# A transformer block with two expert layers: shared expert's blocks overlapped, first weight loads on other queues, three gathered rows a tile, 16 columns of places

## Chip, cores and metric

The kernel runs on one core of a Trainium2 chip, in one launch. The metric is the device time in microseconds; several runs are taken and the median is compared. The profile shown is one further execution, recorded by the hardware profiler.

## The reference

Input x has 4 sequences of 1024 tokens with 256 features, in float32. Four residual layers follow one another; each first normalizes its input over the features.

```
x = x + attn_a(layernorm(x))   # 16 heads of 16; rotary; per-head layernorm; scores ** 4, causal
x = x + ffn(layernorm(x))      # 16 experts of width 176, top 6, plus a shared expert of width 352
x = x + attn_b(layernorm(x))   # a convolution along the first axis, taps from p, q, beta, gamma; silu
x = x + ffn(layernorm(x))      # the same weights again

def ffn(xf):
    shared_out = silu_and_mul(xf @ shared_w1.T) @ shared_w2.T
    probs = softmax(xf @ gate_w.T)
    weights, selected = top_k(probs, 6)          # not renormalized
    moe_out = sum over selected experts of weight * (silu_and_mul(xf @ w1[e].T) @ w2[e].T)
    return moe_out + shared_out
```

attn_b sees the sequences as its first axis, so its convolution is over the four sequences.

## The kernel before

X, the residual stream, stays in SBUF for the whole run, as eight token tiles of 128 positions by four sequences. The tokens are cut into two groups g of four token tiles each.

**Start.** Constants are made on POOL (L137 to L189). SP loads the first half of X in four transfers of 512 KB, one for each sequence (`load_x`, L153). ACT issues eight loads of `w_qkv` of 96 KB and the two tables of rotary angles (L487 to L494). SP then issues 32 tiny loads that replicate the scale and bias of the per-head norm (`lns`, `lnb`, L497 to L502), `w_out`, the second half of X and the gate's weights. The lines outside the hand-ordered part are put in order by a planner, and so they need not run in the order of the text: in the profile `w_out` and one load of X's second half stand before `lns`.

**Attention** (L892 to L938) is ordered by hand: generators ("bites") in lanes are stepped between score blocks. It ends with the routing plan of group 0 and the scatter of its rows into the queue `xq` by indirect DMAs on POOL.

**Expert part** (L941 on). The rows of a group, copied six times each and sorted by expert, fill 111 tiles of 128 rows. `stream` (L1044) walks four stages of 111 tiles: the first expert layer for groups 0 and 1, the second for groups 0 and 1. For each tile, TensorE runs gate and up (`pgu`, L1107), the transposes of the hidden rows (`pht`, L1121), those of a later tile's input (`pxt`, L1076) and the down product (`py`, L1130); ACT and DVE make the activation (`hbuf`, L1115 and L1116), ACT copies out (`hT`, `xgT`, `yo`), and SP loads three tiles (`xg`) and stores three (`yq`) at a time. In the last stage the results go to their places in `z` by an indirect DMA each (L1141), with the row numbers in a column of `zi`; ACT writes a column (L1091), and the eight columns are used in turn. `yo` has two buffers of three tiles.

Beside the tiles, three lanes are stepped: QUEUE holds the weighted sum of the stage before (`combine`) and then the scatter of the stage after (`fill`); SIDE holds convolution, norm, gate and plan; FILL holds the shared expert (`shared`). `combine(g, n, ready)` issues, in each bite, n indirect gathers on POOL into one of three `yg` buffers (L1252), and runs the sums (L1231, on DVE) of the bite two before. A stage's `each` gives QUEUE one bite a tile, so with n = 2 the 96 gathers of a middle stage take 48 tiles, and with SIDE through, the scatter follows with three rows a tile. FILL gets one TensorE bite in each fourth tile.

**Shared expert.** `shared(g, i)` (L985) handles one token tile ("block"): norm on DVE (`hxn`), eight transposes (`hpt`) and two copies on ACT (`hxT`), three times gate and up (`pg`, `pu`), silu on ACT and a product on DVE (`hs`), and the down product in two halves (`po`), each added into X by DVE. All its PSUM tiles rotate through two buffers. For the first stage the four blocks run one after the other ahead of the stream (L1341 and L1342), in the middle stages beside the tiles, and for the last stage in a loop at the end (L1356 to L1361), in which each turn gives one bite to `combine(1, 3, last, True)` and one to FILL. There the rows come from `z` by plain loads on SP (L1250), and `last` finishes a block's FILL bites and stores the block. `Bites.add` (L56) runs a generator up to its first yield at the moment when it is added.

Of the kernel before, what the change touches and what calls it, by code (L numbers as in the profile page):

```python
# [8 lines left out]
FP = mybir.dt.float32  # L9
I32 = mybir.dt.int32  # L10
U32 = mybir.dt.uint32
AF = mybir.ActivationFunctionType
# [13 lines left out]
P = 128  # L26
B, N, E = 4, 1024, 256
# [7 lines left out]
TG = NT // NG  # L35
TT = TG * B
NTILE = TT * TOPK + NEXP - 1
LB = 3
# [68 lines left out]
def block_kernel(  # L107
# [20 lines left out]
    nc = tc.nc  # L128
# [5 lines left out]
    dram = ctx.enter_context(tc.tile_pool(name="dram", bufs=1, space=bass.MemoryType.DRAM))  # L134


    ident = const.tile([P, P], FP, name="ident")  # L137
    make_identity(nc, ident)
    ones = const.tile([P, P], FP, name="ones")
    nc.gpsimd.memset(ones, 1.0)  # L140
    eps_t = const.tile([P, 1], FP, name="eps_t")
    nc.gpsimd.memset(eps_t, EPS)


    X = const.tile([P, NT, B, E], FP, name="X")

    def load_x(l, t):
        nc.sync.dma_start(
            out=X[:, t : t + 4, l, :],
            in_=x[l, t * P : (t + 4) * P, :].rearrange("(t p) e -> p t e", p=P),  # L150
        )

    for l in range(B):  # L153
        load_x(l, 0)


    xq = [dram.tile([NTILE * P, E], FP, name=f"xq{g}") for g in range(NG)]
# [33 lines left out]
    def transpose4(psum_tile, src, cols, rows=P):  # L191

        for i in range(4):
            nc.tensor.transpose(  # L194
                psum_tile[0:rows, i * P : (i + 1) * P], src[:, i, cols], ident
            )
# [12 lines left out]
    def ln_apply(xs, dst, mv, rstd, n=4):  # L209

        for i in range(n):
            nc.vector.tensor_scalar(
                dst[:, i, :],
                xs[:, i, :],
                mv[:, i, 0:1],
                rstd[:, i : i + 1],
                ALU.subtract,
                ALU.mult,
            )
# [255 lines left out]
    with ExitStack() as actx:  # L475
# [10 lines left out]
        wout_sb = ap1.tile([P, 2, E], FP, name="wout_sb")  # L486
        for k in range(2):  # L487
            for g in range(4):
                nc.scalar.dma_start(
                    out=wqkv_sb[:, k, g // 2, :, g % 2, :],  # L490
                    in_=w_qkv[k * P : (k + 1) * P, g, :].rearrange("p (x c) -> p x c", x=3),
                )
        nc.scalar.dma_start(out=cos_sb, in_=cos16.rearrange("(t p) d -> p t d", p=P))
        nc.scalar.dma_start(out=sin_sb, in_=sin16.rearrange("(t p) d -> p t d", p=P))  # L494
        nc.gpsimd.memset(lns, 0.0)
        nc.gpsimd.memset(lnb, 0.0)
        for r in range(G):  # L497
# [443 lines left out]
    with ExitStack() as fctx:  # L941
# [34 lines left out]
        wgu_f = [wgu[:, k].rearrange("p n f -> p (n f)") for k in range(2)]  # L976
        w2_f = [w.rearrange("p n e -> p (n e)") for w in (w2a, w2b)]

        zi = fw.tile([P, 8], I32, name="zi")

        hbuf = [fw.tile([P, 2 * P], FP, name=f"hbuf{i}") for i in range(4)]
        for hb in hbuf:
            nc.vector.memset(hb[:, FI:], 0.0)

        def shared(g, i):  # L985

            t = g * TG + i
            yield "el"
            xn = f1.tile([P, 4, E], FP, name="hxn")
            ln_apply(  # L990
                X[:, t, :, :],
                xn,
                mvs[g][:, 4 * i : 4 * i + 4, :],
                rstds[g][:, 4 * i : 4 * i + 4],
            )
            xT = f1.tile([P, 2, 512], FP, name="hxT")
            yield "pe"
            for k in range(2):
                pt = ps_s.tile([P, 512], FP, tag="s", name="hpt")
                transpose4(pt, xn, slice(k * P, (k + 1) * P))  # L1000
                nc.scalar.copy(xT[:, k, :], pt)
            hs = []
            for s, rows in enumerate(S_ROWS):
                yield "pe"
                pg = ps_s.tile([P, 512], FP, tag="s", name="pg")
                pu = ps_s.tile([P, 512], FP, tag="s", name="pu")
                for dst, gu in ((pg, 0), (pu, 1)):
                    c = gu * FS + s * P
                    for k in range(2):
                        nc.tensor.matmul(  # L1010
                            dst[0:rows, :],
                            lhsT=sh1[:, k, c : c + rows],
                            rhs=xT[:, k, :],
                            start=(k == 0),
                            stop=(k == 1),
                        )
                h = f1.tile([P, 512], FP, name=f"hs{s}")
                nc.scalar.activation(h[0:rows, :], pg[0:rows, :], AF.Silu)
                nc.vector.tensor_mul(h[0:rows, :], h[0:rows, :], pu[0:rows, :])
                hs.append(h)  # L1020
            for pr in range(2):
                yield "pe"
                po = ps_s.tile([P, 2, E], FP, tag="s", name="po")
                for i2 in range(2):
                    l = 2 * pr + i2
                    for s, rows in enumerate(S_ROWS):
                        nc.tensor.matmul(  # L1027
                            po[:, i2, :],
                            lhsT=hs[s][0:rows, l * P : (l + 1) * P],
                            rhs=sh2[0:rows, s, :],  # L1030
                            start=(s == 0),
                            stop=(s == NS - 1),
                        )
                xs = X[:, t, 2 * pr : 2 * pr + 2, :]
                nc.vector.tensor_add(xs, xs, po)

        def shared_all(g):
            for i in range(TG):
                yield from shared(g, i)

        QUEUE, SIDE, FILL = range(3)
        bites = Bites(3)
# [1 line left out]
        def stream(stages):  # L1044
# [35 lines left out]
            def places(c):  # L1080

                st, i = tiles[c]
                if i % LB == 0:
                    _, numbers[:] = nc.values_load_multi_w_load_instructions(
                        plan_of[st][2][0:1, i : i + LB],
                        engines=[ACT],
                        min_val=0,
                        max_val=NEXP - 1,
                        skip_runtime_bounds_check_because="experts' numbers",
                    )  # L1090
                nc.scalar.copy(  # L1091
                    zi[:, c % 8 : c % 8 + 1], xg[c][:, bass.ds(numbers[i % LB] + E, 1)]
                )

            def gate_up(c):
# [30 lines left out]
            def down(c):  # L1126
                st, i = tiles[c]
                py = ps_y.tile([P, E], FP, name="py")
                for k in range(2):
                    nc.tensor.matmul(  # L1130
                        py,
                        lhsT=hT[c][:, k, :],
                        rhs=w2_f[k][:, bass.ds(off[c] * E, E)],
                        start=(k == 0),
                        stop=(k == 1),
                    )
                if i % LB == 0:
                    yo[c // LB] = f2.tile([P, LB, E], FP, name="yo")
                nc.scalar.copy(yo[c // LB][:, i % LB, :], py)  # L1139
                if is_last(st):  # L1140
                    d = nc.gpsimd.indirect_dma_start(  # L1141
                        out=z[:, :],
                        out_offset=bass.IndirectOffsetOnAxis(
                            ap=zi[:, c % 8 : c % 8 + 1], axis=0
                        ),
                        in_=yo[c // LB][:, i % LB, :],
                        in_offset=None,
                    )
# [131 lines left out]
        def again(st):  # L1280

            g = st % NG

            def ready(i):
                bites.add(SIDE, chain(convolve(g * TG + i), prepare(g, i, f1, ps_f)))
                if i == TG - 1:
                    bites.add(SIDE, plan(g, ps_f, st + NG == 3))

            return combine(g, 2, ready)

        def settle():
            for lane in (QUEUE, SIDE, QUEUE, SIDE, QUEUE):
# [45 lines left out]

        with tc.manual_schedule(engines=ORDERED):
            filled.add(0)  # L1340
            bites.add(FILL, shared_all(0))  # L1341
            bites.drain(FILL)  # L1342
            stages = [first, middle(1), middle(2), final]
            stream(
                [
                    (st % NG, lambda st=st: st in filled, force(st), each)
                    for st, each in enumerate(stages)
                ]
            )
            settle()  # L1350

            def last(i):
                bites.need(FILL, i)
                store(TG + i)

            for i in range(TG):  # L1356
                bites.add(FILL, shared(1, i), i)
            bites.add(QUEUE, combine(1, 3, last, True))
            while bites.lanes[QUEUE]:
                bites.begin()  # L1360
                bites.step(9, (1, 0, 1))  # L1361
# [63 lines left out]
```

## Time and profile before

| what | us |
|---|---|
| median of 8 runs | 2477.26 |
| lowest and highest | 2466.48, 2484.55 |
| the profiled execution | 2467.98 |
| its span, first to last instruction | 2466.3 |
| PE busy (share of the span) | 2147.7 (87%) |
| DVE busy | 1110.1 (45%) |
| ACT busy | 1243.4 (50%) |
| POOL busy | 861.5 (35%) |
| mean granted TensorE clock | 0.932 |

PE is TensorE, PEld its weight loads, SP the queue that issues most transfers. Stretches by the profile: attention up to about 736, shared expert of group 0 from 748 to 827, the four stages from there to 1171, 1598, 2024 and 2368, the loop at the end from 2368. A bracket behind a timeline row tells how long the engine sat idle before it and what ended that; a busy share of TensorE is not TensorE at its peak.

### The profile page before, as it was taken

Reading aid. Unit: us, or ns where it says so; the run is one execution under the profiler, and the core shown is the slowest. Engines: PE = TensorE matmul, PEld = TensorE weight load, DVE = VectorE, ACT = ScalarE, POOL = GpSimd, SP = SyncE. Lnnn points to the kernel's source line nnn. Section 1 sums busy time; section 2 is a strip of 40 time slices with the busy share of each in tenths; the row PEclk is TensorE's granted clock in tenths of the full one; section 3 lists DMA queues with packets and bytes.
Section 4 is the critical chain, followed back from the end, with each engine's and each line's share of the span. In section 5 each row is a group of like instructions: output and inputs, shape, how many; then the busy total and the mean of one; then the engine's idle time right before and its main releaser. Section 6 shows DMA issues by size and latency. Waiting matters only on the chain.

```text
span 2466.3 us, 33269 instructions
## 1 busy us (share of the span) xinstructions
PE 2147.7 (87%) x10488; PEld 1329.3 (54%) x10488; DVE 1110.1 (45%) x2610; ACT 1243.4 (50%) x2881; POOL 861.5 (35%) x917
## 2 busy tenths in 40 slices
PE   5879999998938997899889987989998897888996
PEld 2334434333314675677666755666666565666653
DVE  6878877786623341111465611146561112222246
ACT  3768889878821453355454523345553333444420
POOL 3222100005550016610554066255406635656510
PEclk8989999999968999899999998999999899999998
DMA  7980000001126134443454244344424433444445
GB/s 234 340 240 1 1 1 1 1 1 60 67 79 171 39 96 156 160 127 109 143 148 127 78 150 140 113 142 145 126 75 151 160 112 123 131 131 137 125 133 147
DMA packets 230953, 284.90 MB, mean 116 GB/s; under 512 B 39424, under 2 KB 201376, under 8 KB 230784
## 3 DMA queue, kind: packets, MB, share of 16 engines
q1 hardware_dynamic: 184944, 175.44, 23.5%
q0 software_dynamic: 37712, 103.53, 12.8%
q10 hardware_dynamic: 8128, 3.80, 0.7%
q8 instruction: 91, 1.49, 0.3%
q14 instruction: 78, 0.64, 0.1%
HBM read 124.63 MB, written 158.06 MB: 115 GB/s over the span
## 4 chain that ended last, share of the span: by engine, by line
PE 57%; DVE 4%; issue 3%; ACT 3%; another core or an unknown queue 2%; ACTq 0%; DMA 0%; POOL 0%; DVEq 0%
PE pgu L1107 20%; PE py L1130 15%; PE pht L1121 5%; PE pxt L1076 4%; PE pg L1010 4%; PE pu L1010 3%; PE po L1027 3%; DVE X L1231 1%; PE pl L301 1%; PE hpt L194 1%; PE fpt L194 1%; ACT L1115 1%; ACT yo L1139 1%; ACT hT L1123 1%
## 5 line engine op out<-in xcount | busy, mean ns | idle before, releaser
L1107 PE MATMUL pgu<-wgu,xgT 128*128 x1776 | 624.4, 475 | 4.2 <-DVE hbuf L1116 3.2
L1116 DVE TENSOR_TENSOR hbuf<-hbuf,pgu 128x176 f32<-128x176 f32 x444 | 149.3, 337 | 844.3 <-ACT hbuf L1115 661.0
L449 POOL DMA_INDIRECT xq<-sxn,sloti x288 | 290.6, 1009 | 426.8 <-ACT xgT L1078 292.5
L1107 PEld LDWEIGHTS pgu<-wgu,xgT 128*128 128x128 f32 x1776 | 348.1, 197 | 142.0 <-issue 24.6
L1252 POOL DMA_INDIRECT yg<-yq,sloti x288 | 289.8, 1006 | 382.7 <-DMA yq<-yo 178.7
L1115 ACT ACTIVATE hbuf<-pgu 128x176 f32<-128x176 f32 x444 | 142.1, 320 | 420.9 <-PE pgu L1107 286.5
L1130 PE MATMUL py<-w2a,hT 128*128 x888 | 288.5, 408 | 59.0 <-ACT yo L1139 35.7
L754 ACT ACTIVATE s<-ps 128x1024 f32<-128x1024 f32 (+3 forms) x384 | 291.5, 816 | 61.0 <-PE ps L743 55.3
L1139 ACT COPY yo<-py 128x256 f32<-128x256 f32 x444 | 166.8, 376 | 247.9 <-PE py L1130 129.4
L1130 PE MATMUL py<-w2b,hT 128*128 x888 | 275.3, 393 | 0.0
L1121 PEld LDWEIGHTS pht<-ident,hbuf 128*128 128x128 f32 x888 | 124.3, 145 | 199.8 <-issue 85.0
L1121 PE MATMUL pht<-ident,hbuf 128*128 128x128 f32 x888 | 177.9, 283 | 61.9 <-ACT hT L1123 43.4
L774 DVE TENSOR_TENSOR s<-s 128x1024 f32<-128x1024 f32 (+3 forms) x176 | 177.9, 1011 | 52.8 <-ACT s L754 45.5
L1076 PE MATMUL pxt<-ident,xg 128*128 128x128 f32 x888 | 177.6, 283 | 24.9 <-ACT xgT L1078 15.2
L1231 DVE SCALAR_TENSOR_TENSOR X<-yg,top,X 128x256 f32<-128x256 f32 x384 | 185.3, 483 | 25.6 <-DMA yg<-z 11.3
L1078 ACT COPY xgT<-pxt 128x256 f32<-128x256 f32 x444 | 170.1, 383 | 53.1 <-PE pht L1121 24.7
L1130 PEld LDWEIGHTS py<-w2b,hT 128*128 128x128 f32 x888 | 176.1, 198 | 26.3
L1123 ACT COPY hT<-pht 128x256 f32<-128x256 f32 x444 | 166.2, 374 | 39.4 <-PE pgu L1107 12.6
L912 ACT ACTIVATE s<-s 128x1024 f32<-128x1024 f32 (+3 forms) x208 | 169.7, 825 | 27.9 <-DVE s L761 16.0
L1130 PEld LDWEIGHTS py<-w2a,hT 128*128 128x128 f32 x888 | 140.3, 199 | 77.6 <-ACT yo L1139 46.3
L743 PE MATMUL ps<-q,kA 32*128 32x512 f32 (+3 forms) x1024 | 168.7, 602 | 11.8 <-ACT s L754 9.1
L1141 POOL DMA_INDIRECT z<-yo,zi x111 | 110.7, 997 | 89.0 <-ACT hbuf L1115 37.0
(169 smaller groups left out, 2523.9 us busy)
## 6 DMA issues: line engine op xcount, KB each, us to landing
xg<-xq SPq DMA_DIRECT2D x111, 384.0 KB
yq<-yo SPq DMA_DIRECT2D x111, 384.0 KB
xq<-zero SPq DMA_DIRECT2D x36, 768.0 KB
xg<-xz SPq DMA_DIRECT2D x37, 408.0 KB
xz<-zero SPq DMA_DIRECT2D x18, 768.0 KB
yg<-z SPq DMA_DIRECT2D x32, 384.0 KB
wgu<-in_w SPq DMA_DIRECT2D x4, 1408.0 KB
xq<-sxn,sloti POOLq DMA_INDIRECT x288
```

Of the source, the lines that this page charges most:

```text
L449: d = nc.gpsimd.indirect_dma_start(out=queue[:, :], out_offset=bass.IndirectOffsetOnAxis(ap=sloti[:, c + i, k : k + 1], axis=0), in_=xs[:, ...
L754: nc.scalar.activation(s2[:, :, 0:nq], tiles[pr][:, :, 0:nq], AF.Square)
L774: nc.vector.tensor_mul(part, part, part)
L1010: nc.tensor.matmul(dst[0:rows, :], lhsT=sh1[:, k, c : c + rows], rhs=xT[:, k, :], start=(k == 0), stop=(k == 1),)
L1076: nc.tensor.transpose(pt[:, k, :], xg[c][:, k * P : (k + 1) * P], ident)
L1107: nc.tensor.matmul(pg, lhsT=xT[c][:, k, :], rhs=wgu_f[k][:, bass.ds(vals[0] * (2 * FI), 2 * FI)], start=(k == 0), stop=(k == 1),)
L1121: nc.tensor.transpose(pt[:, k, :], hbuf[c % 4][:, k * P : (k + 1) * P], ident)
L1123: d = nc.scalar.copy(hT[c], pt)
L1130: nc.tensor.matmul(py, lhsT=hT[c][:, k, :], rhs=w2_f[k][:, bass.ds(off[c] * E, E)], start=(k == 0), stop=(k == 1),)
L1139: nc.scalar.copy(yo[c // LB][:, i % LB, :], py)
L1231: nc.vector.scalar_tensor_tensor(X[:, t, l, :], yg[:, k, :], top[:, i, k0 + k : k0 + k + 1], X[:, t, l, :], op0=ALU.mult, op1=ALU.add,)
L1252: nc.gpsimd.indirect_dma_start(out=yg[:, k, :], out_offset=None, in_=yq[g][:, :], in_offset=bass.IndirectOffsetOnAxis(ap=sloti[:, i, k0 + ...
```

## The change

Four edits.

1. Start: `ident` is made after `ones` and `eps_t`, and ACT runs one square root on `eps_t` before its loads. Only the first sequence of X is loaded first; the four loads of `w_qkv` with k = 0 go to SP, those with k = 1 stay on ACT; the other three sequences follow on SP; the two tables of angles go to POOL.
2. `shared` gets `ahead`: with it, the next block's norm is issued before a block's three gate and up products, and its transposes and copies between these and the down product. A dictionary `turned` hands the result on, and the tiles of two tags, `h` and `r`, are used in turn (`r` is that of `prepare`). It is on for the first stage and for the loop at the end.
3. The middle stages call `combine` with n = 3.
4. `zi` has 16 columns.

```diff
-    ident = const.tile([P, P], FP, name="ident")
-    make_identity(nc, ident)
     ones = const.tile([P, P], FP, name="ones")
     nc.gpsimd.memset(ones, 1.0)
     eps_t = const.tile([P, 1], FP, name="eps_t")
     nc.gpsimd.memset(eps_t, EPS)
+    root = const.tile([P, 1], FP, name="root")
+    nc.scalar.activation(root, eps_t, AF.Sqrt)
+    ident = const.tile([P, P], FP, name="ident")
+    make_identity(nc, ident)
...
-    for l in range(B):
-        load_x(l, 0)
+    load_x(0, 0)
...
         for k in range(2):
             for g in range(4):
-                nc.scalar.dma_start(
+                (nc.scalar if k else nc.sync).dma_start(
                     out=wqkv_sb[:, k, g // 2, :, g % 2, :],
                     in_=w_qkv[k * P : (k + 1) * P, g, :].rearrange("p (x c) -> p x c", x=3),
                 )
-        nc.scalar.dma_start(out=cos_sb, in_=cos16.rearrange("(t p) d -> p t d", p=P))
-        nc.scalar.dma_start(out=sin_sb, in_=sin16.rearrange("(t p) d -> p t d", p=P))
+        for l in range(1, B):
+            load_x(l, 0)
+        nc.gpsimd.dma_start(out=cos_sb, in_=cos16.rearrange("(t p) d -> p t d", p=P))
+        nc.gpsimd.dma_start(out=sin_sb, in_=sin16.rearrange("(t p) d -> p t d", p=P))
...
-        zi = fw.tile([P, 8], I32, name="zi")
+        zi = fw.tile([P, 16], I32, name="zi")
...
-        def shared(g, i):
+        turned = {}
+
+        def shared(g, i, ahead=False):
+            def norm(i, tag):
+                t = g * TG + i
+                xn = f1.tile([P, 4, E], FP, tag=tag + "xn", name="hxn")
+                ln_apply(
+                    X[:, t, :, :],
+                    xn,
+                    mvs[g][:, 4 * i : 4 * i + 4, :],
+                    rstds[g][:, 4 * i : 4 * i + 4],
+                )
+                return xn, tag
+
+            def turn(xn, tag):
+                xT = f1.tile([P, 2, 512], FP, tag=tag + "xT", name="hxT")
+                for k in range(2):
+                    pt = ps_s.tile([P, 512], FP, tag="s", name="hpt")
+                    transpose4(pt, xn, slice(k * P, (k + 1) * P))
+                    nc.scalar.copy(xT[:, k, :], pt)
+                return xT
+
+            tags = ("h", "r") if ahead else ("h", "h")
             t = g * TG + i
...
+            if (g, i) not in turned:
+                yield "el"
+                normed = norm(i, tags[i % 2])
+                yield "pe"
+                turned[g, i] = turn(*normed)
+            xT = turned.pop((g, i))
+            follows = ahead and i + 1 < TG
+            if follows:
+                yield "el"
+                normed = norm(i + 1, tags[(i + 1) % 2])
             hs = []
             for s, rows in enumerate(S_ROWS):
                 yield "pe"
...
                 hs.append(h)
+            if follows:
+                yield "pe"
+                turned[g, i + 1] = turn(*normed)
             for pr in range(2):
                 yield "pe"
...
-        def shared_all(g):
+        def shared_all(g, ahead=False):
             for i in range(TG):
-                yield from shared(g, i)
+                yield from shared(g, i, ahead)
...
-            return combine(g, 2, ready)
+            return combine(g, 3, ready)
...
-            bites.add(FILL, shared_all(0))
+            bites.add(FILL, shared_all(0, True))
...
-                bites.add(FILL, shared(1, i), i)
+                bites.add(FILL, shared(1, i, True), i)
```

The two uses of `zi` take column `c % 16` instead of `c % 8`.

More of the change, by code (lines that the diff above doesn't have):

```diff
@@ L983, in block_kernel @@
             nc.vector.memset(hb[:, FI:], 0.0)
-        def shared(g, i):
-            t = g * TG + i
[L988 to L1001, printed above, removed]
+        turned = {}
[18 more added lines that the diff above has]
+            tags = ("h", "r") if ahead else ("h", "h")
+            t = g * TG + i
+            if (g, i) not in turned:
[8 more added lines that the diff above has]
+                normed = norm(i + 1, tags[(i + 1) % 2])
             hs = []
@@ L1091, in places @@
                 nc.scalar.copy(
-                    zi[:, c % 8 : c % 8 + 1], xg[c][:, bass.ds(numbers[i % LB] + E, 1)]
+                    zi[:, c % 16 : c % 16 + 1], xg[c][:, bass.ds(numbers[i % LB] + E, 1)]
                 )
@@ L1143, in down @@
                         out_offset=bass.IndirectOffsetOnAxis(
-                            ap=zi[:, c % 8 : c % 8 + 1], axis=0
+                            ap=zi[:, c % 16 : c % 16 + 1], axis=0
                         ),
```

## The prediction

> **What bounds the kernel now.** First the page's head and its chain of waits, then the tiles' times in one middle stage, then the timelines at the three places that the change touches.
>
> ```profile
> span 2466.3 us, 33269 instructions
> ...
> PE 57%; DVE 4%; issue 3%; ACT 3%; another core or an unknown queue 2%; ACTq 0%; DMA 0%; POOL 0%; DVEq 0%
> ```
>
> TensorE holds the end for most of the span, so an edit counts by the TensorE idle time that it removes or makes. The gathers of a middle stage are on POOL and off that chain. The windows of the first middle stage, cut at the starts of yo copies (tiles 0, 48, 64, 104, end):
>
> ```profile
> 1171.50:1349.30 177.80, 163.57 (x737) 115.64 (x736) 101.78 (x263) 88.05 (x230) 97.94 (x96) 0.98 0.49 143
> 1349.30:1404.50 55.20, 52.97 (x253) 40.42 (x252) 35.08 (x125) 31.63 (x78) 0.00 (x0) 0.97 0.27 80
> 1404.50:1575.20 170.70, 145.60 (x563) 97.83 (x563) 29.48 (x74) 56.58 (x168) 93.02 (x96) 0.89 0.40 134
> 1575.20:1597.80 22.60, 22.60 (x109) 17.93 (x109) 3.74 (x9) 9.13 (x28) 0.00 (x0) 1.00 0.30 88
> ```
>
> Columns: length, then busy time of PE, weight loads, DVE, ACT, POOL. In the first row POOL makes the 96 gathers over 48 tiles (3.70 us each), in the second it is idle, in the third it makes 96 scatters (4.27 us a tile, clock 0.89), and the last is tiles and shared expert alone (3.23 us a tile). A tile with nothing beside it takes 2.49.
>
> **The start: weight loads on SP and ACT, X behind them, angles on POOL.** ACT issues ten loads and then loads its table, so the first root waits. Removing that looks like a gain, but something else is next:
>
> ```profile
> 9.87 1.28 ACT L207 ACT_TABLE_LOAD   x1 [9.87 <-DMA wqkv_sb<-in_w_qkv]
> 30.07 0.42 SPq L502 DMA_DIRECT2D lnb<-in_ln_bias  x1
> 32.62 0.78 ACT L675 ACTIVATE kA<-pt,lnb,lns 128x512 f32<-128x512 f32 x1 [2.75 <-PE pt L194]
> DMA  0046999999999999999900000000000000000569
> ```
>
> The last line is the DMA share of the first 34 us in 40 slices. Statistics are done at 7.43 and the root runs at 11.16, so an ACT that is free, with its table already loaded by the early root (1.28 + 0.30 us ahead of its four loads), brings norm, projection, rotation and the scaled q and k 3.7 us forward. But kA also needs lns and lnb, 32 loads on SP, 27 of them 0.46 us apart from 18.15 to 30.49. They land only shortly before 32.62, so at most 0.6 us of the 3.7 can be kept. And SP gets more ahead of them: four weight loads of 96 KB. The DMA engines are full from 3.4 to 17 us at some 300 GB/s (the same answer's rate row), so 384 KB are 1.3 us. Bounds: -0.6, and +5 if the three 512 KB loads of X's second half, now issued after lns (30.53), come to stand before it, since the memset that lns waits for is itself behind the two new issues on POOL (1.5 MB at 300 GB/s). I take +1, by what surely moves. The two POOL issues (0.92 us for the nearest row, raw_de) lie in POOL's idle 6.62 us before 19.06. If the angles land late, the 3.7 us that lns takes away anyway cover them; X's other sequences are first read at 39.12.
>
> [...]
>
> **The shared expert before the stream.** The timeline between two of its four blocks:
>
> ```profile
> 767.98 0.69 DVE L1035 TENSOR_TENSOR X<-X,po 128x512 f32<-128x512 f32 x1 [1.91 <-PE po L1027]
> 768.59 1.38 DVE L212 TENSOR_SCALAR hxn<-X,mvs,rstds 128x256 f32<-128x256 f32 x4
> 769.14 1.64 PE L194 MATMUL hpt<-ident,hxn 128*128 128x128 f32 x8 [1.20 <-DVE hxn L212]
> 771.08 3.48 PE L1010 MATMUL pg<-hxT,sh 128*128 128x512 f32 x4 [0.29 <-ACT hxT L1001]
> ```
>
> From po's end (767.95) to the next pg: 3.1 us. After the change the next block's norm is on DVE before the first product (DVE sits idle 6.67 us there) and its eight transposes stand between the third pu and po. They take 1.04 us unbroken (row at 2367.24). The second four need the PSUM buffer that the third product frees: it starts 0.27 us after pu and takes 0.69, so about 0.5 us of waiting; po's own wait for that product (0.38) is gone. Net -3.1 + 1.04 + 0.5 - 0.4 = -2.0, three times: -6.0. The 3.48 is pg at half rate; at 791.72 it is 1.98, so -1.5 more if that dip goes. Term -7.5 (bounds -4, with the wait doubled and the dip kept, and -8.5). Nothing catches it: transfers are over by 776, and the first expert product comes directly after the last po.
>
> [...]
>
> **The shared expert at the end.** Here the change does not do what it says. All four generators are added before the loop, and `add` runs each to its first yield, past the test of `turned`. So blocks 1 to 3 are normed and turned ahead and then again: three times 4 norms on DVE (1.38), 8 transposes with their weight loads and 2 ACT copies. The serial gap stays.
>
> ```profile
> 2407.99 1.53 DVE L1231 SCALAR_TENSOR_TENSOR X<-yg,top,X 128x256 f32<-128x256 f32 x3
> 2409.99 2.20 PE L194 MATMUL hpt<-ident,hxn 128*128 128x128 f32 x8 [2.76 <-DVE hxn L212]
> 2452.19 4.52 DVE L1231 SCALAR_TENSOR_TENSOR X<-yg,top,X 128x256 f32<-128x256 f32 x9
> 2462.22 0.39 SPq L1268 DMA_DIRECT2D out<-X  x1
> ```
>
> Walking DVE's order. Block 0: the first weighted sums come at 2373.99, when the load lands; a norm (1.38) and another three sums (1.52) now stand before the first product, which holds a PSUM buffer, so TensorE is 2.9 us later; with the ahead turn (1.1 as above) and 0.4 for the products behind it, +4.4. Blocks 1 and 2: the ahead turn +1.1 and some 0.3 behind DVE; but a block is now nine bites instead of seven, so its last po is drained just before the next norm and the three sums of 2407.99 are no longer between: gap 2.76 to 1.3, -1.5 each. That is 2 x -0.1, and -1.0 more because the last of these blocks took 22.6 us against 21.6 through a longer stretch at half rate, which the shorter gap should spare: -1.2. Tail: today six sets of sums follow the last po's addition (2452.27) until the store at 2462.22; with 34 FILL runs instead of 28 only two are left (3.1): -6.9. Together 4.4 - 1.2 - 6.9 = -3.7, taken as -3.5 (bounds -7 and +3: without block 0's loss or without half of the tail's gain).
>
> **Three gathers a tile.** The 96 gathers stay, in 32 tiles instead of 48. Then convolution, plan and scatter come 16 tiles earlier, and 16 tiles without POOL are added at the end: 16 x 3.23 = 51.7 us. A stage was 426.3; the new one is 32x + 426.3 - 177.8 + 51.7, so the break-even is x = 126.1/32 = 3.94 us a tile. What x will be:
>
> ```profile
> 1302.64 0.95 POOL L1252 DMA_INDIRECT yg<-yq,sloti  x1 [0.30 <-issue]
> POOL yg L1252 <- DVE X L1231: 125.3, 68, 4.7
> ```
>
> POOL: 0.95 + 0.30, mean 1.006 + 0.30, so three are 3.75 to 3.92 us; with two a tile it waited for free buffers (second line), with three it hardly will. It sets a floor of about 3.6 to 3.78 a tile (the last sets run past tile 32). TensorE: 32 x 2.49 = 79.7, eight FILL bites at 2.6 (5.09 with one, less 2.49) = 21, convolve and prepare of 2.5 groups at 4.1 (tiles 49 to 57 take 32.0 us, less nine tiles and two bites) = 10, the stall at the first gathers 8: 119 us, 3.7 a tile. The weighted sums wait in DVE's queue before the next tile's hbuf product, so the two chains are coupled, through three buffers. Two equal chains coupled so closely don't overlap fully: I add 6% to 120, x = 3.97, +1 us a stage, +2 in all. Bounds: POOL's floor, -5 to -10 a stage; and the same loop with three scatters a tile, 72.0 us for tiles 72 to 88 (1436.7 to 1508.7), 4.5 a tile, +18 a stage. The nearest row is the same gathers at two a tile, which cost little, hence the low value. The stage's end covers nothing and loses nothing: the scatter is over at 1562.9, 35 us early.
>
> **Sixteen columns.** Column c waits for the scatter of tile c-8; yo's two buffers make ACT wait for that of c-7, so the wider zi only moves the wait. TensorE waited 5.1 us in all for zi: bounds 0 and -5, taken 0.
>
> **Sum.** 1 - 7.5 - 3.5 + 2 + 0 = -8. The profiled execution took 2467.98 us (span 2466.3, 1.7 around it) and would be 2460; the median, 2477.26, lies 9.3 above it: 2469.
>
> **Rivals.** Scatter-like gathers: POOL never pauses, TensorE stalls and drops to half rate as in the scatter window (clock 0.89). At x = 4.5 the middle is +36 and the time 2503. It is slower than before from x = 4.10 (2 x 32 x 0.16 = +10). For it: tiles 2 and 3 of the stage, ten gathers in a row, take 13.0 us instead of 5.0 (yo copies at 1176.43 and 1189.43). Against: quiet tiles with two gathers are at 2.49 with POOL always busy. Late lns: the start at +5, 2473. For it: one X load of the second half already goes before lns. POOL's floor: -10 a stage, 2447 to 2457, about 2453; for it, TensorE's share fits below; against, coupling.
>
> **Chances.** 0.3% is 7.4 us, about what a measurement can tell from none. Forecast 0.42 (faster 0.26, same 0.16; own range 2459 to 2479); scatter-like 0.27 (slower 0.25, same 0.02); late lns 0.15 (faster 0.04, same 0.09, slower 0.02); floor 0.16 (faster). Faster 0.46, same 0.27, slower 0.27. The range 2449 to 2499 leaves out the far half of the scatter-like case and the last of the floor's.
>
> **What would show it.** kA within 1 us of 32.6, or near 37 with late lns; from the first hpt to the first pgu 72 us instead of 79; 76 norm instructions and 152 transposes of the shared expert instead of 64 and 128, and two sets of sums after the last po; tile 32 of a middle stage 121 to 130 us after its tile 0. If that stretch is above 140, the forecast is wrong.

## The result, and the profile after

The changed kernel takes 2533.97 us (median of 17 runs, 2521.45 to 2552.84), the kernel before 2473.59 (46 runs): ratio 1.0252, 95% interval 1.0233 to 1.027. It is 2.5% slower. The profiled execution of after took 2528.6 us (span 2526.9), that of before 2467.98 (span 2466.3). Page of after, its head and the shares of its chain of waits:

```profile
span 2526.9 us, 33300 instructions
...
PE 55%; DVE 5%; issue 4%; another core or an unknown queue 4%; ACT 3%; DMA 0%; POOL 0%; ACTq 0%; DVEq 0%; POOLq 0%; SPq 0%
```

TensorE's share fell by two points and what nobody can name ("issue", "unknown queue") rose from 5% to 8%. Cut at the first yo copy of each stage, the 60.6 us of span go as follows:

| stretch | before | after | difference |
|---|---|---|---|
| start to the last scatter of the attention | 735.7 | 729.9 | -5.8 |
| from there to tile 0 (shared expert before the stream) | 99.1 | 91.9 | -7.2 |
| first expert stage | 336.7 | 341.5 | +4.8 |
| middle stages | 426.3 and 426.0 | 463.8 and 460.1 | +37.5 and +34.1 |
| last stage to the first hpt of the end loop | 343.4 | 345.3 | +1.9 |
| end loop | 99.1 | 94.4 | -4.7 |

The windows of after's first middle stage, cut at tiles 0, 32, 48, 88 and the next stage's tile 0 (length, then busy PE, weight loads, DVE, ACT, POOL, granted clock, DMA share, GB/s):

```profile
1163.30:1323.80 160.50, 120.86 (x493) 83.43 (x493) 90.05 (x226) 62.86 (x156) 96.71 (x96) 0.87 0.44 130
1323.80:1385.20 61.40, 59.53 (x269) 41.50 (x269) 30.09 (x104) 36.93 (x88) 0.00 (x0) 0.97 0.22 69
1385.20:1553.60 168.40, 140.60 (x567) 99.40 (x566) 39.99 (x114) 54.65 (x166) 93.69 (x96) 0.91 0.40 137
1553.60:1627.10 73.50, 73.50 (x333) 53.63 (x332) 11.21 (x28) 32.78 (x97) 0.00 (x0) 1.00 0.28 87
```

The loss is in the first row: 32 tiles with the 96 gathers take 160.5 us (5.02 a tile, 3.70 before). TensorE is idle for 40 of these us and its granted clock is 0.87, POOL is idle for 64. No engine is full. What happens there is seen in the timeline of tile 3, between the yo copies at 1173.19 and 1185.17 (start, length, engine, instruction, in brackets the idle time before it):

```profile
1170.57 1.35 PE L1135 MATMUL pgu<-wgu,xgT 128*128 x4
...
1171.75 0.38 PE L1149 MATMUL pht<-ident,hbuf 128*128 128x128 f32 x2
...
1173.19 0.37 ACT L1167 COPY yo<-py 128x256 f32<-128x256 f32 x1 [2.80 <-PE pxt L1104]
...
1176.02 0.96 POOL L1280 DMA_INDIRECT yg<-yq,sloti  x1 [0.30 <-issue]
1176.75 0.32 ACT L1143 ACTIVATE hbuf<-pgu 128x176 f32<-128x176 f32 x1 [3.19 <-PE pgu L1135]
...
1179.60 0.37 ACT L1151 COPY hT<-pht 128x256 f32<-128x256 f32 x1 [2.53 <-remote]
...
1180.02 0.69 PE L1149 MATMUL pht<-ident,hbuf 128*128 128x128 f32 x2 [4.10 <-issue]
...
1185.06 0.96 POOL L1280 DMA_INDIRECT yg<-yq,sloti  x1 [0.30 <-issue]
1185.17 0.37 ACT L1167 COPY yo<-py 128x256 f32<-128x256 f32 x1 [3.77 <-issue]
```

TensorE's products for pgu end at 1171.92, and ACT, idle but for the copy at 1173.19, starts on them at 1176.75, 4.8 us late (0.04 in a quiet tile); the pht of 1171.75 is copied at 1179.60. (The ends of products are modelled by the profile, so the trace does not tell whether the product itself or the signal of its end is late.) In the other direction nothing is late: that copy ends at 1179.97 and the next pht starts at 1180.02. Nor is it elsewhere: in both profiles no py product starts more than 0.05 us after the ACT copies and TensorE work ahead of it, and no DVE product for hbuf more than 0.03 us after ACT's part and DVE's own work. All the while POOL issues gathers 1.26 us apart, 18 in a row from 1164.6. Some 4 us after the last one starts (1186.3), ACT starts four instructions within 0.8 us. The tile has taken 12 us instead of 2.5.

I took this lateness (end of the four pgu products to ACT's start, only tiles where ACT stood idle for over 0.3 us just before that start: 700 of the 2 x 444 in the two profiles) against the number of gathers and scatters that POOL had started in the 7.6 us before:

| started in 7.6 us | tiles | late by over 1 us | median lateness | longest |
|---|---|---|---|---|
| 0 to 4 | 453 | none | 0.04 us | 0.7 us |
| 5 | 143 | 23% | 0.04 | 6.9 |
| 6 | 104 | 77% | 3.3 | 14.2 |

Six in 7.6 us is a run without a pause, at 1.26 us each. A long lateness here holds part of ACT's own queue, which is late for the same reason; of the tiles where ACT had stood idle since the products' end, none of 458 was late with up to four, 5% of 113 with five and 44% of 45 with six. Before alone shows the same as the table (five: 16% of 70 tiles; six: 80% of 51): this could be read before predicting. With two gathers a tile POOL waited for free buffers after 2 to 12 gathers; three a tile made runs of 15 and 18. Theory for the experiments: **unbroken runs of indirect DMAs on POOL starve what waits for TensorE** (burst theory). Rivals: the three weighted sums crowd DVE ahead of the hbuf product (DVE theory); each gather or scatter costs the others a fixed time wherever it stands; or their traffic slows everything in proportion.

### The profile page after: what moved, and what is told of

It reads as the page before. It is cut to its first block, busy times and chain, and to the rows that moved or that the text cites. A ratio compares the mean times of both kernels' runs of the same rounds, so it can differ in the third digit from the quotient of the medians.

```text
span 2526.9 us, 33300 instructions
## 1 busy us (share of the span) xinstructions
PE 2162.3 (86%) x10512; PEld 1335.2 (53%) x10512; DVE 1116.8 (44%) x2622; ACT 1252.0 (50%) x2888; POOL 864.6 (34%) x919
## 4 chain that ended last, share of the span: by engine, by line
PE 55%; DVE 5%; issue 4%; another core or an unknown queue 4%; ACT 3%; DMA 0%; POOL 0%; ACTq 0%; DVEq 0%; POOLq 0%; SPq 0%
PE pgu L1135 19%; PE py L1158 15%; PE pxt L1104 4%; PE pht L1149 4%; PE pg L1035 3%; PE pu L1035 3%; PE po L1055 3%; DVE X L1259 1%; PE pl L303 1%; PE fpt L196 1%; PE hpt L196 1%; ACT L1143 1%; ACT yo L1167 1%; ACT hT L1151 0%
## 5 line engine op out<-in xcount | busy, mean ns | idle before, releaser
L1167 ACT COPY yo<-py 128x256 f32<-128x256 f32 x444 | 167.0, 376 | 287.6 <-PE py L1158 123.2
```

## The experiments

The runs came in six groups, each from another chip, each beside the kernel before on that chip. They are of two kinds, and this became a result of its own: before took 2472.9, 2475.7 and 2483.2 us in groups 1, 4 and 6 (like the 2473.59 above), and 2283.5, 2281.2 and 2284.3 in groups 2, 3 and 5. I call the first kind starving, for what the runs below show.

### Group 1 (starving): which of the theories

Two gathers a tile again, all else as changed:

```diff
-            return combine(g, 3, ready)
+            return combine(g, 2, ready)
```

> The changed kernel with its middle stages back at two gathers a tile, all else as changed. Burst theory (six or more indirect DMAs back to back on POOL make TensorE's completions reach ACT and PE's own waits some us late; three gathers a tile make bursts of 12 to 18, two a tile rarely more than 6): the two middle stages return to about 426 us each, and what is left of the change is -13 us by the first tile, +5 in the first stage, +2 in the last stage and -5 at the end, so about -11 us against before (ratio 0.995, 2462). DVE theory (three sums a tile ahead of the hbuf product): the same time, since its cause goes too. If another part of the change (16 columns, the shared expert's blocks) is what made the middle stages long, the time stays near 2534.

2455.02 us, ratio 0.9922 (0.9893 to 0.995). Middle stages 423.9 and 421.6. So the three gathers alone made the change slower; the rest of it is a gain of 18 us (by the interval 12 to 26). Sums left out, then gathers left out, in the middle stages:

```diff
-            for k in range(n):
+            for k in range(0 if middle else n):
                 nc.vector.scalar_tensor_tensor(
```

> The changed kernel with the weighted sums of the two middle stages left out (their gathers still run, their rows are added to nothing). Burst theory: POOL is then not held by DVE and runs 96 gathers back to back, 1.26 us apart, 121 us; TensorE's completions are late all that time, the granted clock falls, and tile 32 comes at 145 us or later after tile 0 (160.5 with the sums); total 2500 or more. DVE theory: without the sums nothing stands ahead of the hbuf product, tile 32 comes at 120 us or earlier, total 2455 or less.

```diff
-                    for k in range(0 if placed else n):
+                    for k in range(0 if placed or middle else n):
                         nc.gpsimd.indirect_dma_start(
```

> The changed kernel with the gathers of the two middle stages left out; the weighted sums still run, three a tile, on one buffer that holds zeros. Burst theory: POOL does nothing in that stretch, no completion is late, tile 32 comes at about 105 to 120 us after tile 0, total about 2440 to 2455. DVE theory: three sums a tile still crowd the hbuf product, tile 32 stays at 145 us or later, total 2500 or more.

Without the sums: 2659.06 us, ratio 1.0749 (1.0687 to 1.0811). Without the gathers: 2434.39, ratio 0.9841 (0.9783 to 0.9898). The window of the run without sums, first eight tiles of the first middle stage (138.2 us in the second):

```profile
1155.50:1292.20 136.70, 33.80 (x109) 21.58 (x108) 4.20 (x12) 11.87 (x35) 91.49 (x96) 0.59 0.37 107
```

Eight tiles in 137 us, TensorE busy for a quarter of it, while POOL makes all 96 gathers, none of which waits. ACT's timeline within:

```profile
1189.97 0.37 ACT L1106 COPY xgT<-pxt 128x256 f32<-128x256 f32 x1 [5.22 <-remote]
1201.12 0.37 ACT L1167 COPY yo<-py 128x256 f32<-128x256 f32 x1 [10.77 <-remote]
1212.32 0.58 ACT L1011 COPY hxT<-hpt 128x512 f32<-128x512 f32 x1 [10.83 <-issue]
1224.21 0.58 ACT L1011 COPY hxT<-hpt 128x512 f32<-128x512 f32 x1 [11.31 <-remote]
```

ACT gets on by one instruction in some 11 us, each time after a wait for TensorE. The eight tiles behind, with the gathers over, take 27.6 us. Without the gathers, tile 32 comes 116.3 and 114.6 us after tile 0, sums and all. The DVE theory falls in both runs: taking the sums away made it some 125 us worse than after, because waiting for DVE was what had made POOL pause (13 times, 37.1 us in all, in after's stretch of 160.5; in this run it never does).

Pauses were to be made with three memsets of a scratch tile behind each gather:

> As the run without sums, but with three small memsets on POOL behind each gather (0.2 to 0.3 us each), so that gathers come some 2 us apart instead of 1.26 and 96 of them take some 195 us instead of 121. Burst theory (only six within 7.6 us count: in both profiles no tile with four or fewer in the 7.6 us before it was late by over 1 us): no completion is late although POOL is busier and for longer, tile 32 comes at about 105 to 120 us, total 2440 to 2460, well below the run without sums. Traffic theory (the gathers' bytes and descriptors slow everything in proportion): the same total loss spread over a longer time, total as in the run without sums. DVE theory: as the run without sums, both fast.

2674.0 us, ratio 1.0809 (1.0749 to 1.0869). This run tells nothing new: nothing bound the memsets to the gathers, and the trace has all of them between 732 and 919 us, before the middle stages, and the gathers still 1.26 us apart, eight tiles in 137 us.

### Groups 2 and 3 (not starving)

Memsets into the slot that the gather fills, so that they must come before it:

```diff
+                        if middle:
+                            nc.gpsimd.memset(yg[:, k, :], 0.0)
+                            nc.gpsimd.memset(yg[:, k, :], 1.0)
                         nc.gpsimd.indirect_dma_start(
                             out=yg[:, k, :],
```

> As the run without sums (weighted sums of the middle stages left out), with two memsets of the 128x256 slot on POOL ahead of each gather, some 0.34 us each, bound to the gather by the slot, so that two gathers and 1.3 to 1.5 us of memsets alternate: about 1.95 us a gather, 96 of them in some 190 us. Burst theory (what starves TensorE and ScalarE is POOL making descriptors without a pause; fewer than six indirect DMAs in 7.6 us do no harm): the first eight tiles of a middle stage take about 25 to 30 us instead of 137, tile 32 comes at 105 to 120 us, total 2440 to 2470. Rival (POOL being busy at all is what harms, or each gather costs the others a fixed time): POOL is as busy and for longer, so eight tiles still take over 100 us, total 2660 or more.

2230.15 us, ratio 0.9769 (0.9744 to 0.9794). The first stage's scatter thinned, the middle stages' scatter thinned, and the end loop's blocks normed once (each with two gathers a tile):

```diff
-                bites.add(QUEUE, fill(1, 2))
-            bites.step(1, (2 if i % 8 == 0 else 1, 1, 0))
+                bites.add(QUEUE, fill(1, 1))
+            bites.step(1, (2 if i % 4 == 0 else 1, 1, 0))
```

> The changed kernel with two gathers a tile again, and the scatter of the first expert stage thinned from two a tile (three in every eighth bite's tile) to one a tile with a second in every fourth: 96 scatters over about 77 tiles instead of 43. Burst theory: one scatter in some 2 us stays under six in 7.6 us, so the 43 tiles that took 3.4 to 3.5 us each go to 2.5 to 2.7 and the first stage falls from 341 us to 300 to 315; total 2455 less 25 to 40, 2415 to 2430. Rival (each scatter takes a fixed time from TensorE, some 0.45 us, wherever it stands): the same 96 scatters cost the same 43 us, total 2450 to 2460.

```diff
-                    bites.add(QUEUE, fill(st + 1, 3))
-                bites.step(1, (1, 1, 0))
+                    bites.add(QUEUE, fill(st + 1, 2))
+                    thin.add(st)
+                bites.step(1, (2 if st in thin and i % 4 == 1 else 1, 1, 0))
```

> The changed kernel with two gathers a tile again, and the scatters of the two middle stages thinned from three a tile to two, with a second bite of two in the tiles that carry a bite of the shared expert (5.1 us instead of 2.5): 2.5 a tile, 39 tiles instead of 32. Burst theory: fewer runs of six, the stretch of tiles 64 to 104 falls from 169 us to 145 to 160 a stage; total 2455 less 10 to 40. Rival (a fixed time a scatter): no difference, 2450 to 2460. If the scatter then ends past the stage's last tile, the next stage waits for it and the total rises instead.

```diff
-            if (g, i) not in turned:
-                yield "el"
+            yield "el"
+            if (g, i) not in turned:
```

> The changed kernel with two gathers a tile again, and the test for a block that is already normed and turned put behind the generator's first yield, so that in the end loop blocks 1 to 3 are normed and turned once (ahead) and not twice. By the profile of after each second norm and turn holds TensorE for 2.2 us of transposes, 1.2 to 2.8 us of waiting for the norm and about 1 us until the first product, three times: 9 to 15 us less, total 2440 to 2446. If the end is set by the weighted sums and the loads on SP instead (84 sums of 0.5 us in the end loop stay), no more than 3 us less.

Thinned first stage 2270.64, ratio 0.9942 (0.9922 to 0.9963); thinned middle 2267.81, 0.9939 (0.9919 to 0.9959); once at the end 2260.1, 0.99 (0.988 to 0.9919). Against before at 2283.49 the expected totals had no meaning, but the stages have: the first stage is 298.2 us in all three, thinned or not, every tile 2.49 us beside up to 16 scatters in 8 tiles. Thinning is worth nothing there. The end is worth 10: 87.4 us behind the last tile against 97.5 in the thinned run of the group.

Group 3 therefore asked for the change itself and repeated the pair:

> The changed kernel itself, unedited, because the second group of runs came from a chip on which the kernel before takes 2283 us instead of 2473 and on which no completion was late in runs of 16 and more indirect DMAs. Starvation theory (the cost of three gathers a tile is TensorE and ScalarE being starved by unbroken runs of indirect DMAs, and that happens on some chips only): where before takes some 2283 the change is faster, by 7 + 5 us for the shared expert, 2 to 6 for the start and up to 15 a middle stage (with three a tile the scatter no longer runs past the stage's last tile, which takes 4.8 to 5.5 us a tile there with two): 2230 to 2260, ratio 0.977 to 0.99. Where before takes some 2473 it is slower again, ratio 1.02 to 1.03. Rival (three gathers a tile cost TensorE time everywhere): ratio 1.02 or more on either chip.

> As the run without sums before. Where before takes some 2473: again eight tiles in some 137 us beside 96 gathers without a pause. Where before takes some 2283, by the starvation theory: the same 96 gathers 1.26 us apart, but eight tiles in 21 to 27 us, total 2225 to 2240; by the rival over 2300.

> As the run without sums and with memsets between the gathers, two gathers and then 1 us of memsets (3.47 us for two). Where before takes some 2473, by the burst theory: 4 to 5 gathers in 7.6 us starve little, eight tiles take 25 to 45 us instead of 137, total 2440 to 2480; if POOL's being busy is what harms, eight tiles stay above 100 us, total 2650. Where before takes some 2283: as before, 2230.

> As the run with the first expert stage's scatter thinned to five in four tiles (and two gathers a tile). Where before takes some 2473, by the burst theory: the first stage falls from 341 us to 300 to 315, total 2415 to 2430; if each scatter takes a fixed time, it stays at 2450 to 2460. Where before takes some 2283: 298 as before, ratio about 0.994.

The unedited change: 2265.36 us beside 2281.18, ratio 0.9925 (0.9908 to 0.9941): on this chip it is 0.7% faster. It was expected at 2230 to 2260, with up to 15 us from each middle stage; that gain did not come. Without sums 2224.08, ratio 0.9748 (0.9728 to 0.9767); with pauses 2228.83, 0.9769 (0.9749 to 0.9789); thinned first stage 2272.23, 0.9959 (0.9943 to 0.9974). The run without sums, tiles 0 to 8 of its first middle stage:

```profile
1115.40:1136.10 20.70, 20.70 (x105) 16.10 (x104) 4.00 (x12) 11.46 (x34) 14.81 (x16) 1.00 0.62 185
```

The same program with the same 96 gathers 1.26 us apart: eight tiles in 20.7 us instead of 136.7. In this run and the unedited one, none of 476 tiles with five or more in 7.6 us was late by over 1 us. So the runs of gathers are harmless here, and the change, in its first middle stage (cut at the same tiles 0, 32, 48, 88, end), does this:

```profile
1116.40:1241.90 125.50, 110.50 (x493) 78.12 (x491) 89.60 (x226) 61.73 (x155) 96.22 (x93) 0.96 0.54 163
1241.90:1303.00 61.10, 58.70 (x270) 40.96 (x270) 30.19 (x105) 37.23 (x88) 3.54 (x4) 0.99 0.25 76
1303.00:1426.00 123.00, 122.84 (x567) 91.42 (x566) 40.20 (x114) 54.68 (x166) 75.32 (x78) 1.00 0.51 170
1426.00:1499.50 73.50, 73.50 (x333) 53.65 (x332) 11.20 (x28) 32.75 (x97) 17.81 (x19) 1.00 0.35 118
```

Beside the gathers 160.5 us became 125.5, and in the tiles of the scatter 168.4 became 123.0, at full clock. The other two windows, where the starving chip had no indirect DMA at all, are as long as there (61.1 and 61.4, 73.5 and 73.5). The stage takes 383.1 us, and with two gathers a tile (the thinned run) 383.3: three a tile is worth nothing here either.

### Group 4 (starving): do pauses cure it

> Without sums and with memsets between the gathers, as in the two runs before it, both of which came from chips where nothing starves. Where before takes some 2473, by the burst theory: eight tiles take 25 to 45 us instead of 137, total 2440 to 2480; if POOL's being busy is what harms, eight tiles stay above 100 us, total 2650. Where before takes some 2283: 2230 again.

2436.54 us, ratio 0.984 (0.9781 to 0.9899). POOL's timeline and the window of the first eight tiles:

```profile
1176.52 0.96 POOL L1283 DMA_INDIRECT yg<-yq,sloti  x1 [0.31 <-issue]
1177.47 0.58 POOL L1281 MEMSET yg<- 128x256 f32 x2
1177.97 0.58 POOL L1282 MEMSET yg<- 128x256 f32 x2
1178.72 0.96 POOL L1283 DMA_INDIRECT yg<-yq,sloti  x1 [0.16 <-POOL yg L1282]
1179.98 0.96 POOL L1283 DMA_INDIRECT yg<-yq,sloti  x1 [0.30 <-issue]
```

```profile
1165.10:1193.40 28.30, 24.41 (x105) 18.01 (x104) 4.18 (x12) 11.77 (x35) 22.53 (x38) 0.88 0.52 149
```

Two gathers, 1.2 us in which POOL only runs memsets, two gathers: eight tiles take 28.3 us instead of 137 (20.8 without any gathers), with POOL at work for 80% of them. Not POOL's work harms, but indirect DMAs without a break. (What POOL does in the 0.96 us of one, the traces do not show: the descriptors in the expectations were a guess.) A fixed cost for each gather falls too: the same 192 gathers cost 222 us more when nothing stood between them (2659.06 and 2436.54 us, on two chips of this kind). So does traffic: the quick window moves 149 GB/s, the slow one 107. The three gains joined (two gathers a tile, first scatter thinned, end once):

> Two gathers a tile, the first expert stage's scatter thinned to five in four tiles, and each block of the end loop normed and turned once; the start, the shared expert's blocks ahead and the 16 columns stay as changed. By the starvation theory: where before takes some 2473 it joins -18 (two gathers a tile), -25 to -40 (thinned scatter) and about -10 (end): 2400 to 2435, ratio 0.97 to 0.985. Where before takes some 2283 the thinning is worth nothing and the rest as measured: 2258 to 2262, ratio 0.99. If each scatter takes a fixed time from TensorE wherever it stands, the ratio is 0.985 to 0.99 on either chip.

2403.43 us, ratio 0.9711 (0.9662 to 0.9761), 72 us less than before: -18, -10 and the first stage's -43, which this run shows (25 to 40 had been expected). Tiles 24 to 104 of its first stage, and tiles 24 to 64 of before, where two scatters a tile ran:

```profile
912.60:1111.50 198.90, 198.90 (x961) 152.84 (x960) 31.98 (x94) 103.57 (x321) 93.08 (x96) 1.00 0.51 169
```

```profile
916.70:1055.00 138.30, 114.83 (x485) 81.55 (x484) 18.54 (x54) 51.32 (x160) 86.84 (x90) 0.93 0.50 163
```

With one scatter in 2 us TensorE is busy for all of the 199 us. The first stage is 298.2 us, as on the chips that don't starve, and 341.5 with the same scatters two a tile.

### Groups 5 and 6: the best version

> The joined version with the scatters of the middle stages thinned as well, from three a tile to 2.5 on average (two, and two bites of two in tiles that carry a bite of the shared expert). Where before takes some 2473, by the starvation theory: tiles 64 to 104 of a middle stage fall from 167 us to 145 to 160, so 10 to 40 us in both stages; 2365 to 2395, ratio 0.955 to 0.968. If 2.5 a tile still makes runs of six or more (in tiles of 2.5 us two scatters fill POOL), there is no more than 5 us in it: 2398 to 2405. Where before takes some 2283 nothing is gained: 2258 to 2262.

> The joined version with the scatters of the middle stages at 2.5 a tile, once more, since the run before came from a chip that does not starve (2262 there, as foretold). Where before takes some 2473: tiles 64 to 104 of a middle stage at 145 to 160 us instead of 167, total 2365 to 2395; if 2.5 a tile still makes runs of six or more, 2398 to 2405. Where before takes some 2283: 2262 again, and the question stays open.

Group 5 did not starve: 2261.66, ratio 0.9899 (0.9881 to 0.9918), nothing from the thinning. Group 6 did: 2393.91 us, ratio 0.9639 (0.9612 to 0.9666). Tiles 64 to 104 of the middle stages take 152.2 and 149.7 us (166.7 and 167.0 in the joined run, 126.6 where nothing starves), so some 40% of the loss is gone there. Two scatters in a tile of 2.5 us are still six in 7.6 us, which fits the rest. The whole stages gained less, 412.9 and 418.0 us beside 419.7 and 423.9, since the scatter now reaches past tile 104. This version is faster than before on both kinds of chip, by 3.6% and 1.0%. On starving chips it stands at 0.9639 of before and after at 1.0252; on the others at 0.9899 and 0.9925, with intervals that overlap, so the two are not told apart there.

## Why the prediction was wrong

**The failed step is the price of x, "Three gathers a tile".** I had x = 3.97 us a tile, +1 us a stage. It was 5.02 and 4.99 on the starving chip, and the stages took +37.5 and +34.1. The step added up engine times (119 for TensorE, 120 for POOL, 6% for coupling, a guess that no run shows apart) and so had no place for a wait in which no engine works: in these 160.5 us TensorE stood idle for 40, and what it handed to ACT came up to 14 us late. (A slip within it changes nothing: convolve and prepare come to 4.4 us a group by its own figures, not 4.1.) Where nothing starves x is right: 125.5 us for the stretch against 32 x 3.97 = 127. That the stage comes out even there too, 383.1 against 383.3, is partly luck: up to tile 104 three a tile is 10 us behind (360.5 us, 350.1 with two), and it catches up because with two the scatter runs past the last tile.

**The rival was right in kind and laid aside for a wrong reason.** Scatter-like gathers had x = 4.5 and a chance of 0.27; it was 5.0, and even its 2503 us is 31 too low. Its evidence, tiles 2 and 3 at 13.0 us behind ten gathers, was the mechanism itself. What I set against it, quiet tiles at 2.49 with POOL always busy, holds only for the first five or so gathers of a run (none of 453 tiles late with up to four in 7.6 us, 77% with six): POOL paused 28 times for DVE in that stretch, and I counted these waits as time that three a tile would save. They were what kept TensorE supplied.

**"If that stretch is above 140, the forecast is wrong"** named the place: 160.5.

**Start, +1: sign wrong, small.** kA came at 31.10 instead of 32.62. The lns loads were to hold it at 32.6; but the planner put them ahead of wout and all of X's second half, and they went out from 8.08 on, the last at 25.43 (was 30.07):

```profile
7.37 0.30 ACT L209 ACTIVATE a_rstd<-a_mv,eps_t 128x4 f32<-128x4 f32 x1 [4.53 <-DVE a_mv L206]
...
7.92 3.85 DVE L214 TENSOR_SCALAR xn<-X,a_mv,a_rstd 128x256 f32<-128x256 f32 x4
...
25.43 0.42 SPq L506 DMA_DIRECT2D lnb<-in_ln_bias  x1
...
31.10 0.78 ACT L679 ACTIVATE kA<-pt,lnb,lns 128x512 f32<-128x512 f32 x1 [2.75 <-PE pt L196]
```

The root ran 3.8 us earlier (7.37, was 11.16); the norm took 3.85 us where it took 1.85. Why it did was not tried. Another 4.3 us came off within the attention, where nearly all score products start between 1.3 and 7.9 us earlier than before; no run takes that apart.

**Shared expert before the stream, -7.5: right.** 72.0 us from the first hpt to the first pgu (forecast 72, was 79.35), without the second block's half-rate dip: its pg takes 1.88 (was 3.48). That this dip went was luck: in before the same 1.20 us of idle stands ahead of the third and fourth blocks too, and their pg took 1.98, so the idle alone does not make it.

**End loop, -3.5: right, -4.7.** The blocks are normed twice, as read from the code (152 transposes, 76 norms). Cut at the transposes right before each block's products, block 0 cost 5.5 us more (forecast 4.4), blocks 1 and 2 saved 2.5 (1.2), block 3 and the tail 7.7 (6.9): two sets of sums follow the last addition.

```profile
2518.89 0.69 DVE L1063 TENSOR_TENSOR X<-X,po 128x512 f32<-128x512 f32 x1 [0.48 <-PE po L1055]
2519.61 3.09 DVE L1259 SCALAR_TENSOR_TENSOR X<-yg,top,X 128x256 f32<-128x256 f32 x6
2522.72 0.39 SPq L1296 DMA_DIRECT2D out<-X  x1
```

Done once, the end is worth another 10 us; the forecast saw the duplicates but not that price.

**The first stage, no term: +4.8.** The scatter's last ten went out without a pause, and tiles 63 and 64 took 11.7 us beside them. It need not be a cost of the change: in group 1 the same first stage took 341.5 us in the run with two gathers a tile and 336.7 in the run without sums. **Sixteen columns, 0:** not tried apart.

**The sum.** -8 was forecast; without the three gathers it is -18 on a starving chip, and the whole change is -16 on one that does not starve. Everything but the one step was within 10 us; that step was 70 off, beyond its upper bound of +18 a stage, which came from a loop of scatters that each wait for a tile's copy.

## What to carry to other kernels

A queue of indirect DMAs that never pauses can cost the engines that have nothing to do with it (here eight tiles took 136.7 us, and 28.3 with pauses): look for waits that end with "issue" or an unknown queue, and set them against the number of such DMAs in the microseconds before. Waits of POOL for its buffers are not always waste (the run without those for DVE was some 125 us slower); before removing them, see what the others do in the tiles where POOL had none. Spread scatters thinly over all the tiles there are, rather than have them done early (298.2 us instead of 341.5 for the first stage), and time such a kernel on more than one chip (before took 2473 to 2483 us, or 2281 to 2284).

## What the hardware showed that I had not expected

**Two kinds of chip.** The kernel before takes 2473 to 2483 us in four sets of runs and 2281 to 2284 in three others, 8% apart. The traces of after, one on each kind, have the same instructions and the same POOL pitch (1.26 us). A quiet tile takes 2.49 us on both; the difference lies in the stages with indirect DMAs (first stage 341.5 or 298.2, last stage 345 or 282), and within a middle stage beside them alone. Each of the six chips was used in one group only, so whether the kind belongs to the chip or to the occasion is not shown.

**Six within 7.6 us.** On the starving chip, up to four indirect DMAs of 128 rows (1 KB each) in 7.6 us made no tile late in 453; with six 77% were late; beside an unbroken run of 96 a handover from TensorE to ACT took some 11 us. Only what waited for TensorE was seen late, not what waited for ACT (never over 0.05 us).

**What is behind it stays open.** On the starving chips the traces also lack semaphore updates: 2497 records for TensorE's 2694 in after, 2435 of 2676 in the joined run; on the others they are whole (2692 of 2694, 2675 of 2676). It is not TensorE's alone: in after ACT has 2403 of 2859 and DVE 1997 of 2328, and nothing that waited for ACT was late. They are missing only beside indirect DMAs (after's first middle stage has 287 of TensorE's 326 beside gathers and scatters, and 185 of 185 in its two windows without any), and also where nothing is late: in the joined run's tiles 24 to 104 TensorE has 282 of 320. So missing records and lateness go with the same DMAs but not with each other. All runs of this study were recorded, so whether the recording itself takes part was not tried.
